# Seven products of quarters instead of eight in two fp32 projections, with sums on GpSimd and exponentials by single heads

## Chip, cores and metric

One NeuronCore of a Trainium2 chip. The metric is the device time in microseconds (us) of the whole kernel, the median of several runs. The engines run side by side and each takes its instructions strictly in its own order: TensorE (PE in the profile; its weight loads PEld) multiplies matrices into PSUM, VectorE is DVE, ScalarE is ACT, GpSimd is POOL, and SyncE (SP) issues most DMA transfers. GpSimd works on SBUF alone; VectorE and ScalarE read PSUM too.

## What is computed

A gated transformer block over 4096 tokens (2 batches of 2048) of width 512: cross-attention with 16 heads of 32 to 77 context tokens, then a feed-forward layer with simulated int8 rounding.

```python
def _L0_xattn_ref(query, key, value, Wq, bq, Wk, bk, Wv, bv, Wo, bo):
    q = proj(query, Wq, bq)          # y = x @ W.T + b, split into 16 heads
    k = proj(key, Wk, bk)
    v = proj(value, Wv, bv)
    scores = jnp.einsum('bhqd,bhkd->bhqk', q, k) / jnp.sqrt(jnp.float32(D_K))
    attn = jax.nn.softmax(scores, axis=-1)
    ctx = jnp.einsum('bhqk,bhkd->bhqd', attn, v)
    return ctx.transpose(0, 2, 1, 3).reshape(B, Sq, D_MODEL) @ Wo.T + bo

def _qlinear(x2d, w, b):             # round(x / sx) @ round(w / sw).T, scaled back
    ...

x = x + tanh(g_xattn) * _L0_xattn_ref(_layernorm(x), ctx, ctx, ...)
x = x + tanh(g_ffn) * _L0_ffn_ref(_layernorm(x), w1, b1, w2, b2)   # _qlinear, gelu, _qlinear
```

`sx` is the largest magnitude of the whole layer input, so the feed-forward half can't begin before all tokens have passed the attention half.

## The kernel before

**Blocks and steps.** The tokens are cut into 8 blocks of 512 (index `i`), each of 4 tiles of 128 (`t`). The 16 heads form 4 groups of 4 (`g`). The attention half is a loop over blocks and, in each, 8 steps `s`: step `s` belongs to group `s // 2` and to one half (256 tokens) of the block. It is software-pipelined by two steps. In step `s` the kernel issues, in this order:

- `apply_v` in even steps (L404): the shares of the group before times the values, into PSUM, copied to `cT` by ScalarE (L412);
- `scores` for two steps ahead (L352) into `ps` (two banks, two buffers), with the maximum over each head (`mx`, L361) and the subtraction of it (`e`, L363) on VectorE;
- `transpose_a` (L395): the shares of this step, transposed in two tiles on TensorE, copied to `aT` by ScalarE (L396);
- `exponential` for two steps ahead on ScalarE, one instruction for 616 columns (L373);
- `shares` for two steps ahead: sum and reciprocal on VectorE (`sm` L380, `rs` L382) and the multiply on GpSimd (L384);
- a quarter of a projection: `project_o` of the block before in even steps (L420), `project_q` of this or the next block in odd ones (L332). A projection of a block is 16 fp32 matmuls of 128x512 for the queries (4 groups of 4) and 16 for the output (4 tiles of 4).

Around these lie the layer norm's statistics of later blocks (`norm_stats`) and of finished ones (`norm2_stats`, `norm2_max`), `add_bias` (L327, GpSimd: the output bias into the residual), `scale_x` (L289, GpSimd: the transposed input from block 2 on times 1/sigma), and weight tasks with fixed steps: the maxima of w1 and w2 (L465), their rounding on ScalarE (L481) and conversion to bf16 on VectorE (L489) into `w1q` and `w2q`, which stay in SBUF.

**Order.** In the attention half the program order is kept for TensorE, VectorE and ScalarE (`tc.manual_schedule`, L511); GpSimd's and the DMA queues' order is chosen by the scheduler, with hints (`tc.issue_after`).

**PSUM.** `ps_s` has 2 buffers for scores, `ps_t` 2 for transposes, `ps_p` 2 for all projections and `apply_v`.

**Feed-forward half** (from L720): bf16 matmuls `ph` (L738), gelu on ScalarE, maxima on VectorE; the hidden values are stored to HBM but for the last 10 tiles; then `pf` (L805) from `w2q`. Its inputs are transposed by DMA (L717) one block ahead.

## Time and profile before

| what | value |
|---|---|
| time, median of 3 runs | 638.99 us (638.86 to 639.27) |
| the profiled run's own time | 640.32 us |
| span of the profiled execution | 638.5 us, 8087 instructions |
| attention half up to the first `ph` | 404.9 us |
| fp32 matmuls of the output projections, L420 | 115.1 us busy, 264 records |
| fp32 matmuls of the query projections, L332 | 86.6 us + 29.3 us busy |
| mean granted TensorE clock | 0.991 |

Times are in us unless marked ns. An fp32 matmul leaves two records, one for each pass. In a line of the timeline the first number is the start from the span's begin, the second the length, then engine, source line, operation, result and operands, shape, and count; in brackets the idle time before it and what ended it. In a line of a group the numbers after the bar are busy us, mean ns of one, idle us of the engine before them and what ended that. "busy" of TensorE counts modelled ends of pipelined matmuls, so neighbours overlap in the list.

### The profile page before, as it was taken

How to read it: one execution, taken by the hardware profiler on the slowest of the kernel's cores; microseconds unless marked ns; L12 is line 12 of the kernel's file. 1: busy time of each engine (PE TensorE's matmuls, PEld its weight loads, DVE VectorE, ACT ScalarE, POOL GpSimd, SP SyncE). 2: the span in 40 equal slices, each digit the busy share in tenths (PEclk: the TensorE clock that was granted, in tenths of full speed). 3: DMA queues.
4: the chain of work that ended last, by engine and by line, in shares of the span. 5: the costliest groups of instructions: out<-in, count | busy, mean ns of one | idle time of the engine just before them, and what ended most of it. 6: DMA issues, size and time to landing. Idle time of an engine off the chain costs nothing.

```text
span 638.5 us, 8087 instructions
## 1 busy us (share of the span) xinstructions
PE 615.9 (96%) x2957; PEld 311.5 (49%) x2978; DVE 509.0 (80%) x796; ACT 341.0 (53%) x450; POOL 247.2 (39%) x202
## 2 busy tenths in 40 slices
PE   5999999999999999999999999799999979999997
PEld 5556555455545554555545555344444424444444
DVE  5688777889898997887857787899999789877452
ACT  2255444563434654544344442598989879556510
POOL 2145457465355364273362341000000009998000
PEclk9999999999999999999999999799999989999999
DMA  9921510442520232220000000199999109798932
GB/s 282 371 97 52 119 42 26 114 168 78 136 66 1 84 131 67 82 68 2 16 1 1 1 17 0 51 337 302 346 331 294 20 24 380 271 376 315 399 129 82
DMA packets 50542, 90.66 MB, mean 142 GB/s; under 512 B 22139, under 2 KB 26491, under 8 KB 44872
## 3 DMA queue, kind: packets, MB, share of 16 engines
q1 hardware_dynamic: 49400, 89.48, 42.8%
q10 hardware_dynamic: 1104, 0.69, 0.4%
q8 instruction: 23, 0.38, 0.2%
q14 instruction: 15, 0.12, 0.1%
HBM read 55.01 MB, written 31.47 MB: 135 GB/s over the span
## 4 chain that ended last, share of the span: by engine, by line
PE 81%; DVE 15%; ACT 1%; POOL 1%; issue 1%; DMA 1%; DVEq 0%
PE ph L738 17%; PE pf L805 17%; PE po L420 13%; PE pq L332 13%; PE pta L395 8%; PE ps L352 6%; PE pc L404 4%; DVE e L363 2%; DVE mx L361 2%; DVE sm L380 1%; DVE st_a L163 1%; DVE max_w L465 1%; PE pk L226 1%; DVE xmax L445 1%; PE pvv L250 1%; DVE x L430 1%
## 5 line engine op out<-in xcount | busy, mean ns | idle before, releaser
L384 POOL TENSOR_TENSOR e<-e,rs 128x616 f32<-128x616 f32 x64 | 81.7, 1277 | 164.4 <-DVE rs L382 77.2
L396 ACT COPY aT<-pta 77x512 f32<-77x512 f32 x128 | 68.2, 583 | 99.4 <-PE pta L395 99.4
L420 PE MATMUL po<-wo_sb,cT 128*128 128x512 f32 (+1 forms) x264 | 115.1, 580 | 0.0
L805 PE MATMUL pf<-w2q,hq 128*128 128x512 bf16 (+1 forms) x518 | 112.0, 376 | 2.9 <-DVE hq L208 2.1
L738 PE MATMUL ph<-xqT,w1q 128*128 128x512 bf16 x501 | 112.0, 383 | 2.6 <-DVE xqT L208 1.8
L746 ACT ACTIVATE G<-ph,b1s,s 128x512 f32<-128x512 f32 x128 | 99.4, 777 | 13.8 <-PE ph L738 2.9
L332 PE MATMUL pq<-xT,wq_sb 128*128 128x512 f32 x192 | 86.6, 593 | 0.2 <-POOL xT L289 0.2
L756 DVE TENSOR_REDUCE hmax<-G 128x1 f32<-128x1024 f32 (+1 forms) x65 | 77.0, 1198 | 7.2 <-ACT G L746 7.1
L805 PEld LDWEIGHTS <-hq 128*128 128x128 bf16 x528 | 51.9, 99 | 62.9 <-DVE hq L208 3.0
L738 PEld LDWEIGHTS <-w1q 128*128 128x128 bf16 x512 | 50.6, 99 | 63.9 <-issue 4.9
L380 DVE TENSOR_REDUCE sm<-e 128x8 f32<-128x616 f32 x64 | 50.3, 787 | 25.9 <-ACT e L373 25.9
L420 PEld LDWEIGHTS po<-wo_sb,cT 128*128 128x128 f32 x264 | 47.8, 190 | 47.5 <-issue 46.2
L395 PE MATMUL pta<-ident,e 128*77 128x128 f32 x512 | 70.2, 280 | 0.6 <-POOL e L384 0.6
L373 ACT ACTIVATE e<-e 128x616 f32<-128x616 f32 x64 | 45.9, 718 | 44.2 <-DVE e L363 42.0
L361 DVE TENSOR_REDUCE mx<-ps 128x8 f32<-128x616 f32 x64 | 50.6, 791 | 17.2 <-PE ps L352 16.9
L395 PEld LDWEIGHTS pta<-ident,e 128*77 128x77 f32 x512 | 55.6, 147 | 11.4 <-issue 9.4
L798 ACT ACTIVATE Gb<-Gb,inv_h 128x2048 f32<-128x2048 f32 x22 | 43.6, 1999 | 32.4 <-DMA Gb<-h 32.4
L352 PEld LDWEIGHTS ps<-kb,qT 64*128 64x128 f32 x512 | 36.0, 186 | 46.9 <-ACT qT L340 23.1
L819 POOL TENSOR_TENSOR x<-x,b_sb 128x512 f32<-128x512 f32 x32 | 57.2, 1823 | 0.1
L363 DVE TENSOR_TENSOR e<-ps,mx 128x616 f32<-128x616 f32 x64 | 51.2, 800 | 6.7 <-DVE mx L361 0.5
L332 PEld LDWEIGHTS pq<-xT,wq_sb 128*128 128x128 f32 x192 | 34.5, 190 | 35.0 <-issue 33.5
L827 DVE SCALAR_TENSOR_TENSOR x<-pf,s,x 128x512 f32<-128x512 f32 (+1 forms) x33 | 23.7, 730 | 34.4 <-PE pf L805 28.4
(101 smaller groups left out, 666.2 us busy)
## 6 DMA issues: line engine op xcount, KB each, us to landing
h<-G SPq DMA_DIRECT2D x22, 1024.0 KB, 6.0
Gb<-h SPq DMA_DIRECT2D x22, 1024.0 KB, 7.9
out_y<-x SPq DMA_DIRECT2D x31, 256.0 KB, 3.2
x<-in_x SPq DMA_DIRECT2D x7, 1024.0 KB, 7.4
xT<-in_xT SPq DMA_DIRECT2D x6, 1024.0 KB, 5.5
raw_w<-in_w2T SPq DMA_DIRECT2D x6, 1024.0 KB, 5.5
raw_w<-in_w1T SPq DMA_DIRECT2D x4, 1024.0 KB, 12.5
rrow<-row SPq DMA_DIRECT2D x6, 256.0 KB, 4.8
```

Of the source, the lines that this page charges most:

```text
L332: nc.tensor.matmul(pq, wq_sb[:, kc, g * P : (g + 1) * P], (xnT if i < 2 else xT_sb)[i][:, kc, :], start=(kc == 0), stop=(kc == KC - 1),)
L352: nc.tensor.matmul(ps[:, q, u * RK : (u + 1) * RK], qT[i, g][r, t * P : (t + 1) * P], kblk[i // NBB][r, g, :], start=True, stop=True,)
L361: nc.vector.tensor_reduce(mx, sc, AX.X, ALU.max)
L363: nc.vector.tensor_tensor(e.rearrange("p u (q r k) -> p q u r k", q=NR, r=RT), sc, mx[:, :, :, :, None].to_broadcast([P, NR, 2, RT, NK]), ...
L384: return nc.gpsimd.tensor_tensor(e4, e4, rs[:, :, :, None].to_broadcast([P, 2, HG, NK]), ALU.mult).ins
L395: nc.tensor.transpose(pt[:NK, j, :], es[i, s][:, u, j, :], ident)
L396: nc.scalar.copy(aT[i, g][:, :, t * P : (t + 1) * P], pt[:NK, :, :])
L420: nc.tensor.matmul(po[i, t, c.start][:, : c.stop - c.start], cT[i, g][:, t * P : (t + 1) * P], wo_sb[:, g, c], start=(g == 0), stop=(g == ...
L738: nc.tensor.matmul(ph[u], w1q[:, kc, fc * P : (fc + 1) * P], cur[:, kc, :], start=(kc == 0), stop=(kc == KC - 1),)
L746: nc.scalar.activation(G[:, 2 * v + u, :], ph[u], AF.Gelu, bias=b1s[:, fc : fc + 1], scale=s1,)
L756: nc.vector.tensor_reduce(hmax[:, k + u : k + u + 1], G[:, 2 * v + u : 2 * v + u + n, :], AX.XY, ALU.max, apply_absolute_value=True,)
L805: nc.tensor.matmul(po[t, c.start][:, : c.stop - c.start], hq[:, fc, t * P : (t + 1) * P], w2q[:, fc, c], start=(fc == 0), stop=(fc == FC - 1),
```

## The change

**Products of quarters.** For the query projections of blocks 2 to 7 and the output projections of blocks 0 to 6, the 512x512x512 product is written as seven products of 256x256x256 quarters (Strassen's algorithm in Winograd's form) instead of eight. `product` issues the four fp32 matmuls of 256 columns of one of them. Units 0, 2, 4, 6 add up in one PSUM bank, units 1, 3, 5 in another; after each unit the running sum is read out: for the queries (`unit_q`) by ScalarE with the bias (units 0, 2, 3, 6) or by VectorE as an addition to what is there (1, 4, 5), for the output (`unit_o`, `add_unit`) by VectorE into the residual. The next unit of a bank has to wait for that reading.

The sums of quarters that feed the products are made on GpSimd: `sums_x` and `sums_c` (four each for every block, 128x512), `sums_wq` and `sums_wo` (four each, once). The units stand in tables by step (`plan`; `second` for block 1, `begin` for block 0, `end` for block 7). `("o", n)` is output unit n of the block before, `("O", 0)` that of this block, `("q", n)` query unit n of the next; `p` and `P` are old `project_q` calls. The last unit of a step has its addition at the start of the next step (`waiting`).

**Exponentials.** The subtraction on VectorE is dropped. VectorE multiplies the maxima by -SCALE (`nmx`), and ScalarE takes the exponential of each head and tile straight from PSUM with that as its bias, eight instructions of 77 columns for a step instead of one of 616. So the scores' PSUM buffer is read until the exponentials end.

**Moved with it.** `apply_v` writes to `ps_t` instead of `ps_p`; `ps_p` becomes two banks used in turn. Statistics and maxima of the norms, centring of wq, `load_x` and `spread_rstd` change their steps. `w2q` is no longer kept through the attention half: its four converted pieces pass through `xqT0` to HBM (`w2_dram`), and one DMA of 2 MB brings them back at the start of the feed-forward half, ahead of the first transposes in SP's queue. GpSimd joins the engines whose program order is kept.

```diff
+    w2_dram = rows.tile([P, FC, D], BF16, tag="w2", name="w2_dram", bufs=1)
...
+        def sums_c(i, n):
+            a11, a21 = (quarter(cT[i, 0], 0, r) for r in range(2))
+            s = ct_s[i, n] = piece(f"cs{i}_{n}")
+            if n == 3:
+                combine(s, a11, a21, ALU.subtract)
+                return
+            a12, a22 = (quarter(cT[i, 1], 0, r) for r in range(2))
+            if n == 1:
+                combine(s, a21, a22, ALU.add)
+            elif n == 2:
+                combine(s, ct_s[i, 1], a11, ALU.subtract)
+            else:
+                combine(s, a12, ct_s[i, 2], ALU.subtract)
+
+        def product(ps, a, b, more=False):
+            for m in range(2):
+                for c in range(2):
+                    nc.tensor.matmul(
+                        ps[:, m * H : (m + 1) * H],
+                        a[:, c, m * P : (m + 1) * P],
+                        b[:, c, :],
+                        start=(m + c == 0 and not more),
+                        stop=(m + c == 2),
+                        skip_group_check=True,
+                    )
...
+            if n in (0, 2, 3, 6):
+                for m in range(2):
+                    g = 2 * r + m
+                    nc.scalar.activation(
+                        q[:, m, :], ps[:, m * H : (m + 1) * H], AF.Identity, bias=bq_sb[:, g : g + 1]
+                    )
+            else:
+                nc.vector.tensor_tensor(q, ps.rearrange("p (m t) -> p m t", m=2), q, ALU.add)
+
+        def unit_o(i, n):
+            pa, pb = chain(("o", i))
+            ct = [cT[i, c] for c in range(2)]
+            a, b = (
+                (quarter(ct[0], 0, 0), quarter(wo_sb, 0, 0)),
+                (quarter(ct[1], 0, 0), quarter(wo_sb, 1, 0)),
+                (ct_s.get((i, 2)), wo_t[:, 1]),
+                (ct_s.get((i, 1)), wo_t[:, 0]),
+                (ct_s.get((i, 3)), wo_t[:, 2]),
+                (ct_s.get((i, 4)), quarter(wo_sb, 1, 1)),
+                (quarter(ct[1], 0, 1), wo_t[:, 3]),
+            )[n]
+            product(pb if n in (1, 3, 5) else pa, a, b, more=n in (2, 4, 5, 6))
...
-            e = work.tile([P, 2, GK], F32, tag="e", name=f"e{n}", bufs=3)
-            nc.vector.tensor_tensor(
-                e.rearrange("p u (q r k) -> p q u r k", q=NR, r=RT),
-                sc,
-                mx[:, :, :, :, None].to_broadcast([P, NR, 2, RT, NK]),
-                ALU.subtract,
-            )
+            nmx = small.tile([P, NR, 2, RT], F32, tag="nmx", name=f"nmx{n}")
+            nc.vector.tensor_scalar(nmx, mx, -SCALE, None, ALU.mult)
...
-            return nc.scalar.activation(e, e, AF.Exp, scale=SCALE).ins
+            for u in range(2):
+                for q in range(NR):
+                    for r in range(RT):
+                        j = q * RT + r
+                        last = nc.scalar.activation(
+                            es[i, s][:, u, j * NK : (j + 1) * NK],
+                            sc[:, q, u, r, :],
+                            AF.Exp,
+                            bias=nmx[:, q, u, r : r + 1],
+                            scale=SCALE,
+                        )
...
-            pc = ps_p.tile([P, TB], F32, tag="pp", name=f"pc{i}_{g}")
+            pc = ps_t.tile([P, TB], F32, tag="pt", name=f"pc{i}_{g}")
...
+            dst = w1q[:, :, j * TB : (j + 1) * TB] if name == "w1" else xqT0
             nc.vector.tensor_scalar(dst, wraw[name, j], MAGIC, None, ALU.subtract)
+            if name == "w2":
+                nc.sync.dma_start(w2_dram[:, j * KC : (j + 1) * KC, :], xqT0)
...
+        plan = {
+            0: [("o", 1)],
+            1: [("o", 2), ("o", 3)],
+            2: [("o", 4), ("o", 5)],
+            3: [("o", 6), ("q", 0)],
+            4: [("q", 1), ("q", 2)],
+            5: [("q", 3), ("q", 4)],
+            6: [("q", 5)],
+            7: [("q", 6), ("O", 0)],
+        }
+        begin = {1: [("p", 2)], 3: [("p", 3)], 5: [("P", 0)], 6: [("P", 1)], 7: [("P", 2)]}
+        end = {s: [("o", s + 1)] for s in range(6)}
...
+                if waiting:
+                    add_unit(*waiting)
+                    waiting = None
                 if ahead[0] < NB:
                     scores(*ahead)
...
+                if i > 0 and s == 1:
+                    sums_c(i - 1, 2)
+                d = 2 if i == 1 else 1
+                if i > 0 and more and s == d + 3:
+                    sums_x(i + 1, 2)
...
                 if ahead[0] < NB:
-                    last = shares(*ahead)
+                    shares(*ahead)
+                for n, (kind, unit) in enumerate(units.get(s, ())):
...
+                if i > 0 and s == 0:
+                    sums_c(i - 1, 1)
+                if i > 0 and s == 1:
+                    sums_c(i - 1, 4)
+                if more and i > 0:
+                    if d <= s < d + 2:
+                        for kc in range(2):
+                            scale_x(i + 1, 2 * (s - d) + kc)
+                    if s == d + 2:
+                        sums_x(i + 1, 3)
+                        sums_x(i + 1, 1)
+                    if s == d + 4:
+                        sums_x(i + 1, 4)
+                if more and s == 7:
+                    sums_c(i, 3)
+                t = s - NT if i == 0 else s // 2
+                if t >= 0 and (i == 0 or s % 2 == 0):
+                    add_bias(i, t)
...
+    w2q = late.tile([P, FC, D], BF16, name="w2q")
+    nc.sync.dma_start(w2q, w2_dram)
```

## The prediction

> **What bounds the kernel now.** I read the engine totals, then the chain of work that ended last, then the busy time of one block of the attention half, and last the timeline inside it.
>
> ```profile
> PE 615.9 (96%) x2957; PEld 311.5 (49%) x2978; DVE 509.0 (80%) x796; ACT 341.0 (53%) x450; POOL 247.2 (39%) x202
> ...
> PE 81%; DVE 15%; ACT 1%; POOL 1%; issue 1%; DMA 1%; DVEq 0%
> ```
>
> TensorE is busy nearly throughout and holds 81% of the chain. One block, from one `apply_v` of step 0 to the next:
>
> ```profile
> 253.50:299.00 45.50, 45.50 (x227) 23.31 (x226) 36.48 (x65) 21.25 (x33) 21.93 (x20) 1.00 0.17 53
> ```
>
> The columns after the length are TensorE, its weight loads, VectorE, ScalarE, GpSimd: TensorE has no gap in 45.5 us, VectorE is at 80%, GpSimd at 48%. Two steps in order of time:
>
> ```profile
> 248.31 0.80 PE L352 MATMUL ps<-kb,qT 64*128 64x154 f32 x8
> 249.03 1.10 PE L395 MATMUL pta<-ident,e 128*77 128x128 f32 x8
> 249.15 0.80 DVE L361 TENSOR_REDUCE mx<-ps 128x8 f32<-128x616 f32 x1
> 249.97 3.60 PE L332 MATMUL pq<-xT,wq_sb 128*128 128x512 f32 x8
> 250.05 0.80 DVE L363 TENSOR_TENSOR e<-ps,mx 128x616 f32<-128x616 f32 x1
> 250.88 0.72 ACT L373 ACTIVATE e<-e 128x616 f32<-128x616 f32 x1
> 251.63 0.80 DVE L380 TENSOR_REDUCE sm<-e 128x8 f32<-128x616 f32 x1 [0.78 <-ACT e L373]
> 252.47 0.20 DVE L382 RECIPROCAL rs<-sm 128x8 f32<-128x8 f32 x1
> 252.84 1.22 POOL L384 TENSOR_TENSOR e<-e,rs 128x616 f32<-128x616 f32 x1 [1.81 <-DVE rs L382]
> ```
>
> Starts are first. From scores to the GpSimd multiply it is 4.53 us (248.31 to 252.84), and nobody waits for it, since those shares are transposed two steps later. So TensorE bounds, and what shortens it pays only as long as nothing else makes it wait.
>
> **The change, part by part.**
>
> *Products.* Four 512-column matmuls take 3.44 us in the chain (249.97 to the next work is 3.53), 0.86 each, so a projection of 16 is 13.76. A 256-column one is half, 0.43; the 128x256 row of L420 gives 3.6 us for 8, 0.45. A product of four is 1.72, seven are 12.04. Query of blocks 2 to 7 and output of blocks 0 to 6 make 13 projections: 13 x 1.72 = -22.4 us of TensorE (-15 at 0.45). I take 0.43.
>
> *Exponentials.* VectorE loses the subtraction (64 x 0.80) and gains `nmx`; ScalarE gets eight 128x77 instructions for one of 0.72. The nearest row is the 32x77 one with a bias column:
>
> ```profile
> L242 ACT ACTIVATE kb<-pk,bk_sb 32x77 f32<-32x77 f32 x8 | 2.5, 318 | 6.2 <-DVE kb L244 6.2
> L396 ACT COPY aT<-pta 77x512 f32<-77x512 f32 x128 | 68.2, 583 | 99.4 <-PE pta L395 99.4
> L170 DVE TENSOR_SCALAR ve_f<-mean 128x2 f32<-128x2 f32 x13 | 7.8, 600 | 0.5
> L170 DVE TENSOR_SCALAR ve_a<-mv 128x4 f32<-128x4 f32 x7 | 1.2, 169 | 0.2
> ```
>
> Two copies of 583 ns end within 1.07 us, so neighbours overlap by 0.095: eight take 8 x 0.223 + 0.095 = 1.88 us. Ends: 1.5 (from the 203 ns of the one-column `warm`, plus 0.064 for 77 elements by the slope of the copies) and 2.5 (no overlap). I take 1.88. The Trainium skill ("ScalarE: Activation LUTs", What ACT_TABLE_LOAD costs) gives 280 ns plus 0.833 ns an element with a bias pointer and 93 ns of overlap; an estimate from it is 2.10 us, which would add about 3 us to the whole sum. `nmx` is 0.17 by the `ve_a` row, 0.60 by `ve_f`: the same instruction, which there sits until a GpSimd instruction ends (253.48 to 254.08, GpSimd's multiply being at work from 252.84). New latency from scores to multiply: 0.84 + 0.91 + 0.20 + 1.88 + 0.03 + 0.83 + 0.37 = 5.06 us, the unchanged links from the timeline above. ScalarE gains 512 x 0.223 - 46 = 68 us and stays under 80% of a block; VectorE's account is -51 + 11 (`nmx`) + 18 query additions at 0.69 (the 77x512 `vb` row) + 21 more output additions at 0.73 = -12 us. Neither is the bound by its total.
>
> *GpSimd sums: where TensorE now waits.* 60 new sums of 128x512 at 1.27 us (the L327 and L289 rows): 76 us, mostly in blocks 1 to 6, GpSimd from 48% to some 70%. The total fits; the order does not. In steps 0 and 1 of a block GpSimd's queue reads: multiply of this step's scores, first sum (`sums_c` 1), `add_bias`, second sum (`sums_c` 2). TensorE's queue from the same scores on: transposes, unit 1, scores, transposes, unit 2, and unit 2 reads the second sum. GpSimd is done 5.06 + 1.18 + 1.23 + 1.23 + 1.27 = 9.97 us after the scores began. TensorE arrives after 0.73 + 0.93 + 1.81 + 0.73 + 0.93 = 5.13. It waits 4.9 us, and all behind it does (unit 3, `apply_v`, the next scores). Both chains begin at the same scores, so no slack built up elsewhere helps. It happens in blocks 2 to 7; in block 1 unit 2 comes a step later.
>
> *Second wait.* Scores 1 of the next block (step 7) read the query sum that VectorE writes after unit 5 (step 6). VectorE gets to it only after that step's maximum, the eight exponentials, sum and reciprocal: 4.69 + 0.12 + 0.69 + 0.1 = 5.6 us after the scores; TensorE has 0.73 + 0.93 + 1.81 = 3.5 of work: 2.1 us of wait. In step 5 the query addition and two `norm2_stats` follow the reciprocal and make VectorE 0.5 late: 2.6. Blocks 2 to 6; about 0.8 in block 1.
>
> *Third.* Unit 2 of the queries waits for `sums_x` 2, fourth behind a multiply: 9.97 against 9.66 of TensorE work, 0.3 us.
>
> So a block 2 to 6 needs 42.0 + 4.9 + 2.6 + 0.3 = 49.8 us (45.5 - 2 x 1.72 = 42.0). Before, these five ran from 115.89 to 344.55 in the list of the chain: 228.7. Now 249: **+20.5**.
>
> *Port.* Each `nmx` can sit behind a GpSimd instruction, up to 1.2 us. Following GpSimd's queue through a block, it is at work when `nmx` is due in steps 0, 4, 5 and 6, which feed the two waits: about +1.9 a block, 6 blocks, **+11** (0 to +24).
>
> *Clock.* TensorE now stands still 11 times for 2.6 us or more.
>
> ```profile
> 396.91 2.72 PE L666 MATMUL px<-ident,xs 128*128 128x128 f32 x16
> 402.27 0.79 PE L185 MATMUL pg_x<-diag_x,ones 128*128 128x128 f32 x2 [2.65 <-DVE diag_x L178]
> 404.89 1.44 PE L738 MATMUL ph<-xqT,w1q 128*128 128x512 bf16 x3 [1.82 <-DVE xqT L208]
> ```
>
> and the busy time in stretches of 4 us, the third column from the end being the granted clock:
>
> ```profile
> 404.00:408.00 4.00, 2.89 (x7) 1.13 (x8) 3.93 (x10) 1.21 (x2) 0.56 (x1) 0.50 0.00 0
> 408.00:412.00 4.00, 4.00 (x18) 1.67 (x16) 4.00 (x7) 3.56 (x5) 0.00 (x0) 0.87 0.23 39
> ```
>
> After standing 2.65 and 1.82 us TensorE runs at clock 0.50 until about 409, 6.8 us; after 2.17 and 1.75 at 519 it is 3.4 us. A 3.4 us stretch at half clock loses 1.7 us. Ends: nothing, and 3.4 for each of 11 waits, 37. I take 1.7 for six long waits and half for five short: **+14**. The Trainium skill ("TensorE: Matmul & The Clock Gate", Part 1: The HAM clock gate) wants an idle window of about 3.4 us before the clock halves; by it only the six long waits count, an estimate of +10. It speaks against this change either way.
>
> *The rest.* Block 0 gets a fifth projection (+3.4); block 1 has 47.0 us of TensorE work against 46.6, the 0.8 and more VectorE work: +3 (0 to 6). In block 7 shorter projections are met by the 4.9 wait and VectorE's chain: 0 (-5 to +2). The weight maxima and roundings of blocks 2 to 5 lie on VectorE (L465: 1.19 each), where it waits anyhow; what spills over: +3 (0 to 10). w2 goes out in four writes and comes back in one read of 2 MB ahead of the transposes in SP's queue; 1024 KB land in 5.5 to 6.0 us, and 409.5 to the first use of the second transposes near 420 is cover: 0 (up to 5).
>
> Sum on the 638.5 us span: 20.5 + 11 + 14 + 3.4 + 3 + 0 + 3 = +55, 693. The profiled run reports 640.32, the median of the runs is 638.99; the difference on the median gives 694, and I forecast **692**.
>
> **Rivals.**
> - *The waits alone* (no port, clock or spill): 639 + 20.5 + 3.4 = 663, and 657 at the short exponentials; 652 to 672. For it: every link is in the rows. Against it: the half clock is in this trace.
> - *VectorE and ScalarE fall behind step after step*: port waits at 4 us a block and the clock twice as dear, 712 and up. For it: VectorE's chain in steps 4 to 6 has no slack. Against: it is idle during the long wait.
> - *TensorE stays the bound, faster*: 639 - 22.4 = 617. One mechanism decides, the wait of output unit 2 in step 1: the gain survives only if GpSimd's second sum ends within 5.1 us of the scores, not 10. Even at no cost for the exponentials (8.1) it does not; only sums at a third of 1.27 would do it. The break-even lies where that wait falls to about 1.5 us and the second to none.
> - *The effects cancel*, 638 to 652: the lower end of each.
>
> **How the numbers follow.** My case (672 to 712) 62%, waits alone 20%, falling behind 11%, faster 5%, cancelling 2%. The range 660 to 716 reaches into the two slower neighbours and leaves out about 2 in 10. Runs of before agree within 0.07%, so 0.2% is about what can be told from no change. Faster 0.05, same 0.01, slower 0.94.
>
> **What would show it.** TensorE idle before output unit 2, about 5 us in each of blocks 2 to 7, released by GpSimd's `cs`; idle before scores, released by VectorE's `qT`, some 2 to 4 us five times; eight exponentials in 1.9 us; clock 0.5 after the long waits; blocks 2 to 6 at 50 to 56 us. It is wrong if those blocks run at 42 to 45 us, or if `cs` is ready before TensorE asks.

## The result and the profile after

The changed kernel takes 737.66 us (median; 736.01 to 741.93) where the kernel before takes 638.92: a ratio of 1.156, 95% interval 1.150 to 1.161. That is 98.7 us slower; the forecast was 53 us slower, 692 us, and its range ended at 716. The profiled execution has a span of 734.2 us against 638.5. Its engine totals, its granted clock in 40 slices, and the chain of work that ended last:

```profile
PE 632.3 (86%) x3269; PEld 391.5 (53%) x3290; DVE 526.5 (72%) x834; ACT 412.4 (56%) x922; POOL 324.7 (44%) x261
...
PEclk9989999989999889989998998898999999999999
...
PE 56%; DVE 21%; ACT 11%; POOL 9%; issue 2%; DMA 0%; ACTq 0%; DVEq 0%; POOLq 0%
```

TensorE has lost its place as the bound: 81% of the chain before, 56% now. Although it has less to multiply, it is busy 16.4 us longer (615.9 before), and it stands idle 101.9 us instead of 22.6. Both have to be explained. Busy time by stretches, block 4 (with weight tasks) and block 5 (nearly without); columns as before, the clock third from the end:

```profile
259.88:323.48 63.60, 48.30 (x273) 36.02 (x272) 44.57 (x76) 33.31 (x95) 35.69 (x28) 0.89 0.29 96
323.48:378.82 55.34, 46.01 (x274) 34.85 (x273) 37.56 (x69) 29.94 (x93) 32.41 (x28) 0.94 0.10 34
```

Each was 45.5 us before. From one first `apply_v` to the next the eight blocks (0 to 7) grew by 11.1, 11.6, 16.8, 12.4, 18.1, 9.8, 11.5 and 3.9 us; the feed-forward half by 0.5. What TensorE waited for (us in total, times, the longest):

```profile
PE oa L432 <- POOL cs L369: 33.9, 7, 6.3
PE ps L508 <- DVE qT L474: 19.7, 6, 5.9
PE qa L432 <- POOL xt L369: 11.3, 5, 3.2
...
PE pta L559 <- ACT cT L577: 6.6, 6, 2.4
```

These are the three waits of the forecast and one more. The first in order of time, block 4, the end of step 0 and step 1:

```profile
263.44 1.83 ACT L530 ACTIVATE e<-ps,nmx 128x77 f32<-128x77 f32 x8
...
264.36 0.80 PE L508 MATMUL ps<-kb,qT 64*128 64x154 f32 x8
...
265.08 1.10 PE L559 MATMUL pta<-ident,e 128*77 128x128 f32 x8
265.30 0.80 DVE L544 TENSOR_REDUCE sm<-e 128x8 f32<-128x616 f32 x1 [0.79 <-ACT e L530]
...
266.50 1.99 POOL L548 TENSOR_TENSOR e<-e,rs 128x616 f32<-128x616 f32 x1 [3.19 <-ACT aT L560]
...
268.46 1.25 POOL L369 TENSOR_TENSOR cs<-cT,cT 128x512 f32<-128x512 f32 x1
...
269.68 1.26 POOL L337 TENSOR_TENSOR x<-x,bo_sb 128x512 f32<-128x512 f32 x1
...
270.90 1.44 POOL L369 TENSOR_TENSOR cs<-cs,cT 128x512 f32<-128x512 f32 x1
...
272.39 1.22 PE L432 MATMUL oa<-wo_t,cs 128*128 128x256 f32 x2 [6.21 <-POOL cs L369]
```

GpSimd's queue runs as foreseen: multiply, first sum, bias, second sum; only then can TensorE go on, 6.2 us late. The eight exponentials take 1.83 us (1.88 foreseen). Behind such a wait, the busy time in stretches of 4 us:

```profile
268.00:272.00 4.00, 0.00 (x0) 0.00 (x0) 3.93 (x6) 2.16 (x9) 4.00 (x4) 0.75 0.89 286
272.00:276.00 4.00, 3.61 (x9) 2.89 (x10) 0.84 (x2) 1.55 (x1) 3.29 (x4) 0.50 0.28 107
```

The clock falls while TensorE stands still and is still 0.50 when it begins again: its next product takes some 3.6 us instead of 1.73. The trace records 90.8 us at half clock (13.1 before), of which 2.0 (2.1) lie behind the last instruction; TensorE was busy in 75.4 of them (7.8 before). If half of the busy time at half clock is lost, that is 37.7 against 3.9 us, **33.8 us more** (an estimate from the two busy times). With that the account of the 95.7 us of span is 79.3 (idle) + 33.8 (clock) - 17.4. The last term is not measured here, it is what is left, and stands for less work; `best3` below gives 17.5 for it in another way.

The new and lengthened instructions of the softmax, as groups (busy us, mean ns of one, idle before them and what ended it), first the sum in the kernel before, then three groups of the changed one:

```profile
L380 DVE TENSOR_REDUCE sm<-e 128x8 f32<-128x616 f32 x64 | 50.3, 787 | 25.9 <-ACT e L373 25.9
```

```profile
L530 ACT ACTIVATE e<-ps,nmx 128x77 f32<-128x77 f32 x512 | 116.5, 340 | 51.9 <-DVE nmx L519 51.6
...
L544 DVE TENSOR_REDUCE sm<-e 128x8 f32<-128x616 f32 x64 | 50.8, 793 | 78.7 <-ACT e L530 78.3
...
L519 DVE TENSOR_SCALAR nmx<-mx 128x8 f32<-128x8 f32 x64 | 32.3, 504 | 2.2
```

VectorE waits 78.3 us for the exponentials (25.9 before), ScalarE 51.6 us for `nmx`, and `nmx`, 0.17 us at its shortest, takes 0.50 on average. Of the 64 the 24 that meet no GpSimd instruction take 0.17 us, and all 30 that take more than 0.3 us end 0.03 us behind the end of a GpSimd instruction. The chain of waits in block 4, steps 2 to 4, is this loop:

```profile
281.76 1.72 ACT e L530 x8
...
283.50 0.81 DVE sm L544
...
284.33 0.20 DVE rs L546
284.54 0.62 DVE x L496
285.15 2.14 DVE xqT L650
287.29 0.66 DVE x L496
287.95 0.72 DVE mx L517
...
288.69 0.99 DVE nmx L519
...
289.76 1.83 ACT e L530 x8
```

ScalarE, then VectorE for 6 us (a weight task of 2.14 in it), then ScalarE again, in the time of one step. While ScalarE works VectorE stands, and what it has still to do comes later.

### The profile page after: what moved, and what is told of

It reads as the page before. It is cut to its first block, busy times and chain, and to the rows that moved or that the text cites. A ratio compares the mean times of both kernels' runs of the same rounds, so it can differ in the third digit from the quotient of the medians.

```text
span 734.2 us, 9354 instructions
## 1 busy us (share of the span) xinstructions
PE 632.3 (86%) x3269; PEld 391.5 (53%) x3290; DVE 526.5 (72%) x834; ACT 412.4 (56%) x922; POOL 324.7 (44%) x261
## 4 chain that ended last, share of the span: by engine, by line
PE 56%; DVE 21%; ACT 11%; POOL 9%; issue 2%; DMA 0%; ACTq 0%; DVEq 0%; POOLq 0%
PE ph L968 15%; PE pf L1035 15%; ACT e L530 8%; PE oa L432 5%; PE pta L559 4%; PE qa L432 4%; PE ps L508 3%; DVE sm L544 3%; PE ob L432 3%; PE pq L342 3%; POOL cs L369 2%; DVE mx L517 2%; DVE nmx L519 2%; POOL e L548 2%; ACT aT L560 2%
## 5 line engine op out<-in xcount | busy, mean ns | idle before, releaser
L548 POOL TENSOR_TENSOR e<-e,rs 128x616 f32<-128x616 f32 x64 | 79.4, 1240 | 194.1 <-DVE rs L546 137.3
L530 ACT ACTIVATE e<-ps,nmx 128x77 f32<-128x77 f32 x512 | 116.5, 340 | 51.9 <-DVE nmx L519 51.6
L560 ACT COPY aT<-pta 77x512 f32<-77x512 f32 x128 | 69.8, 586 | 74.9 <-PE pta L559 74.6
L544 DVE TENSOR_REDUCE sm<-e 128x8 f32<-128x616 f32 x64 | 50.8, 793 | 78.7 <-ACT e L530 78.3
L559 PE MATMUL pta<-ident,e 128*77 128x128 f32 x512 | 77.6, 296 | 8.9 <-ACT cT L577 6.6
L559 PEld LDWEIGHTS pta<-ident,e 128*77 128x77 f32 x512 | 60.2, 157 | 23.3 <-issue 9.7
L508 PE MATMUL ps<-kb,qT 64*128 64x154 f32 x512 | 52.6, 326 | 20.9 <-DVE qT L474 19.7
L432 PE MATMUL oa<-wo_t,cs 128*128 128x256 f32 x112 | 37.3, 492 | 33.9 <-POOL cs L369 33.9
L1026 POOL TENSOR_SCALAR b_sb<-b_sb,s 128x512 f32<-128x512 f32 x1 | 3.5, 3497 | 123.1 <-issue 123.1
L577 ACT COPY cT<-pc 128x512 f32<-128x512 f32 x32 | 19.1, 598 | 62.6 <-PE pc L568 62.5
L432 PEld LDWEIGHTS oa<-wo_t,cs 128*128 128x128 f32 x112 | 26.6, 250 | 40.0 <-POOL cs L369 35.5
```

The lines of the kernel that those rows point to most:

```text
L432: nc.tensor.matmul(ps[:, m * H : (m + 1) * H], a[:, c, m * P : (m + 1) * P], b[:, c, :], start=(m + c == 0 and not more), stop=(m + c == 2 ...
L508: nc.tensor.matmul(ps[:, q, u * RK : (u + 1) * RK], qT[i, g // 2][r, g % 2, t * P : (t + 1) * P], kblk[i // NBB][r, g, :], start=True, sto ...
L530: last = nc.scalar.activation(es[i, s][:, u, j * NK : (j + 1) * NK], sc[:, q, u, r, :], AF.Exp, bias=nmx[:, q, u, r : r + 1], scale=SCALE,)
L544: nc.vector.tensor_reduce(sm, e4, AX.X, ALU.add)
L548: return nc.gpsimd.tensor_tensor(e4, e4, rs[:, :, :, None].to_broadcast([P, 2, HG, NK]), ALU.mult).ins
L559: nc.tensor.transpose(pt[:NK, j, :], es[i, s][:, u, j, :], ident)
```

## The experiments

Three theories. **A**: TensorE's operands come late by the order on GpSimd and VectorE, and the array then runs at half clock. **B**: the longer loop of VectorE and ScalarE in each step sets the time. **C**: small VectorE instructions (`nmx`, `xf`, integers) are held up by GpSimd's work beside them. Times are medians; ratios to the kernel before, measured alongside (638.8 to 640.1 us), with 95% intervals.

### One part alone or undone

`e_whole` takes the exponentials back to the old form: `nmx` out, VectorE subtracts into SBUF, one exponential of 616 columns (8 of 77; the forecast below has 1232).

```diff
-            nc.vector.tensor_scalar(nmx, mx, -SCALE, None, ALU.mult)
+            nc.vector.tensor_tensor(e..., sc, mx..., ALU.subtract)
...
-            (eight activations of 77 columns)
+            return nc.scalar.activation(e, e, AF.Exp, scale=SCALE).ins
```

> The change without its part on the exponentials: VectorE subtracts the maxima into SBUF again and ScalarE takes one exponential of 1232 columns, so that the small product on VectorE (nmx) is gone and ScalarE loses about 0.9 us a step. Theory A (GpSimd and VectorE deliver operands of the products late, and the array then works at half clock): the operands are as late as before, 725 to 750 us. Theory B (the longer serial loop VectorE, ScalarE, VectorE of each step sets the time): 690 to 715 us, and VectorE's idle time behind the exponentials falls from 78 us to about 26. Theory C (VectorE's small SBUF instructions wait for a port that GpSimd holds): nmx's 32 us go and 0.75 us of subtraction a step comes for it, 715 to 735 us.

706.1 us, 1.103 (1.100 to 1.106): 31.5 us less. VectorE's idle time behind the exponentials fell to 20.6 us. This is B's span.

`before_single` puts only the eight exponentials and `nmx` into the kernel before.

```diff
-            nc.vector.tensor_tensor(e..., sc, mx..., ALU.subtract)
+            nc.vector.tensor_scalar(nmx, mx, -SCALE, None, ALU.mult)
...
-            return nc.scalar.activation(e, e, AF.Exp, scale=SCALE).ins
+            (eight activations of 77 columns, bias=nmx[...], scale=SCALE)
```

> The kernel before with the eight single exponentials and nmx alone, no product of quarters. Theory A: TensorE keeps its order and nearly its time, 636 to 650 us. Theory B: the loop is longer by some 0.6 us in 64 steps and decides, 660 to 685 us. Theory C: little GpSimd work lies beside it, nmx stays near 0.2 us; 636 to 650 us as under A.

653.5 us, 1.021 (1.019 to 1.023): 13.4 us, between the forecasts. No product of quarters and no GpSimd sum is in it, so the exponentials cost something by themselves. `nmx` takes 0.55 us on average here too, and C was wrong to expect 0.2: all 31 that take more than 0.3 us end 0.03 us behind a GpSimd instruction, of work that was always there. The wait list of VectorE shows nearly the same time behind the exponentials as in the changed kernel:

```profile
DVE sm L388 <- ACT e L374: 74.5, 47, 2.4
```

`cs_early` issues the two sums behind the longest wait ahead of the multiply.

```diff
+                if i > 0 and s == 0:          # ahead of shares(*ahead)
+                    sums_c(i - 1, 1)
+                    sums_c(i - 1, 2)
-                if i > 0 and s == 1:
-                    sums_c(i - 1, 2)
```

> The changed kernel with the two sums cs_1 and cs_2 issued on GpSimd ahead of the multiplication of step 0, instead of behind it and in step 1. Theory A: TensorE's 33.9 us behind cs_2 go, with most of the half clock behind them (7 waits of up to 3.4 us lost); 685 to 705 us. Theory B: TensorE then stands at the next scores or transposes instead, 722 to 738 us. Theory C: the same GpSimd work holds the same port, 700 to 715 us (the wait goes, the stretched VectorE stays).

707.6 us, 1.106 (1.102 to 1.109): 30.1 us less. The wait is gone from the list but for 1 us, and the waits for `qT` (19.6) and `xt` (12.5) are as before; the one for `cT` grew from 6.6 to 12.4, and `nmx` from 0.50 to 0.62 us on average. Time at half clock fell from 90.8 to 57.0 us. That is just beyond A's span and in C's: the wait is gone, and part of the gain came back as another.

`no_sums` leaves all sums of `sums_x` and `sums_c` out and takes unsummed quarters, so its outputs are not those of the block.

```diff
         def sums_x(i, n):
+            xt_t[i, n] = {1: b12, 2: b22, 3: b22, 4: b21}[n]
+            return
...
         def sums_c(i, n):
+            ct_s[i, n] = quarter(cT[i, int(n > 2)], 0, n % 2)
+            return
```

> The changed kernel without the eight sums of each block (products take unsummed quarters in their place, so the outputs are not those of the reference; all matrix products and additions remain). Theory A: cs, xt and most of the half clock go, and qT stays (19.7 us and its clock); 655 to 680 us. Theory B: 700 us or more. Theory C: as A, and also nmx, xf and the integers on VectorE come back to the durations of before, which makes the blocks with weight tasks as short as the others; 640 to 660 us.

687.5 us, 1.074 (1.072 to 1.077), between A and B. Even with no sums of these two kinds it is 47 us slower than the kernel before (640.1 beside it). So GpSimd's order is only half of the matter, and C's prediction that the durations come back fails: `nmx` still takes 0.52 us on average, beside multiplies, scalings and biases, which were all there before.

### The sums of a step moved past the next maxima

`defer` issues the sum, reciprocal and multiply of a step one step later, right behind the next scores' maxima. The shares are not transposed before the step after that, so the move is free in principle, and VectorE never needs the exponentials of its own step.

```diff
                 if ahead[0] < NB:
                     scores(*ahead)
+                if pending:
+                    shares(*pending)
+                pending = ahead if ahead[0] < NB else None
...
-                if ahead[0] < NB:
-                    shares(*ahead)
```

`before_single_defer` does it in the kernel before with single exponentials; `defer_early` does it in the changed kernel with `cs_1` and `xt_2` ahead of the multiply and `cs_2` right behind; `early_whole` is `cs_early` with the old exponentials. The order in `defer_early`, behind the scores:

```diff
+                if i > 0 and s == 0:
+                    sums_c(i - 1, 1)
+                if i > 0 and more and s == d + 3:
+                    sums_x(i + 1, 2)
+                if pending:
+                    shares(*pending)
+                pending = ahead if ahead[0] < NB else None
+                if i > 0 and s == 0:
+                    sums_c(i - 1, 2)
```

> The kernel before with the single exponentials, and each step's sums, reciprocals and multiplication issued one step later, right behind the next step's maxima, so that VectorE never stands behind the exponentials of its own step. Theory B (the serial loop VectorE, ScalarE, VectorE costs the 13.4 us that the single exponentials cost alone): 636 to 643 us, with VectorE's 75 us of waiting for e nearly gone. Theory C (the lengthened nmx and the other work on VectorE cost them): 648 to 656 us as without the move.

647.6 us, 1.012 (1.007 to 1.017). The median is between the two forecasts (the profiled execution is the longest of the runs, 649.9 us), so the blocks have to decide. Two of them, 3 and 4:

```profile
168.08:213.79 45.71, 45.71 (x228) 23.68 (x227) 38.52 (x75) 27.58 (x88) 23.00 (x21) 1.00 0.31 67
213.79:259.28 45.49, 45.49 (x225) 23.30 (x224) 35.43 (x66) 32.73 (x91) 22.81 (x20) 1.00 0.31 99
```

TensorE has no gap again (49.3 and 47.1 us without the move), and VectorE's wait for `e` is 1.7 us. So the middle blocks no longer pay for the exponentials. The move did two things at once, though: `nmx` now meets a GpSimd instruction only 9 times instead of 44 and is short again. Without the move, and with it:

```profile
L363 DVE TENSOR_SCALAR nmx<-mx 128x8 f32<-128x8 f32 x64 | 35.2, 550 | 2.2
...
L363 DVE TENSOR_SCALAR nmx<-mx 128x8 f32<-128x8 f32 x64 | 13.1, 204 | 2.2
```

So how much of the gain is the wait for `e` (B) and how much the shorter `nmx` (C) this run doesn't separate. The move itself costs 3 us each in block 0 (75.3 against 72.2) and block 7 (64.0 against 60.9), where no later work hides the multiply.

> The changed kernel with the same move of the sums and the multiplication by one step and nothing else. Theory B: the loop cost about the 31 us that the whole exponential gave back, and the addition for q unit 5 is no longer behind it (19.7 us of TensorE behind qT go); the wait for cs_2 stays; 685 to 710 us. Theory A: only qT goes, and cs_2 is as late as before or later; 715 to 730 us. Theory C: 720 to 738 us.

708.7 us, 1.109 (1.105 to 1.114): 29.0 us less, at the upper edge of B's span. The wait for `qT` fell from 19.7 to 8.8 us, the one for `cs` only from 33.9 to 28.4; `nmx` fell here too, from 0.50 to 0.37 us on average.

> Both: the move, and on GpSimd cs_1 ahead of the multiplication of step 0, cs_2 right behind it, xt_2 ahead of that of its step. Theories A and B together: both costs go, with the half clock behind them: 650 to 675 us. If the gains overlap: 680 to 700 us. What stays in any case is block 0's 11 us and the weight tasks.

661.9 us, 1.035 (1.031 to 1.039): 75.7 us less, more than the 59.1 of the two moves alone (xt_2's wait also fell, to 3.8). Blocks 5 and 6 take 43.8 and 44.0 us, for the first time less than the 45.5 of the kernel before.

> The changed kernel with cs_1 and cs_2 early and with the exponential of a whole step as before. If the two gains (30.1 us and 31.5 us) are separate: 675 to 682 us. If they overlap: 690 to 705 us.

676.8 us, 1.059 (1.056 to 1.063): 60.9 less, where the two alone gave 30.1 and 31.5. The two gains are separate and nearly add.

### What `nmx` costs

`after_min` and `defer_min` need no `nmx`: K and its bias are multiplied by -SCALE when they are placed, VectorE takes a minimum, which is already the bias, and the exponential has scale -1.

```diff
-            nc.vector.tensor_reduce(mx, sc, AX.X, ALU.max)
-            nc.vector.tensor_scalar(nmx, mx, -SCALE, None, ALU.mult)
+            nc.vector.tensor_reduce(mx, sc, AX.X, ALU.min)
...
-                    nc.vector.tensor_scalar(dst, pk[r, :NK], bias, None, ALU.add)
+                    nc.vector.tensor_scalar(dst, pk[r, :NK], -SCALE, bias, ALU.mult, ALU.add)
```

> The changed kernel without nmx: the factor -SCALE is put into K and its bias once, VectorE takes minima in place of maxima, and the eight exponentials take these as their bias with scale -1. Theory C (nmx, stretched from 0.17 us to as much as 1.29 us by GpSimd, is a main part of the loss): its 32 us of VectorE lie in the serial loop, so 700 to 715 us. Theories A and B (order, not nmx): 718 to 733 us, since at most the loop's 0.5 us a step goes where VectorE is the last to come.

720.9 us, 1.127 (1.124 to 1.131): 16.8 us less for 32.3 us of VectorE. In A's and B's span: C is a part, not the main one.

> The kernel with both moves (sums one step later, GpSimd's order mended; 661.9 us) and without nmx in the same way. If VectorE bounds blocks 2 to 4 (33 to 44 us busy a block of 48 to 51): each of them loses 2 to 4 us, 648 to 656 us in all. If GpSimd and the waits for q unit 5 bound them: 658 to 663 us.

645.4 us, 1.011 (1.007 to 1.014): 16.5 us less once more, beyond the forecast. Block 3 fell from 48.5 to 43.8, block 4 from 50.8 to 47.8.

### The half clock by itself

`after_fill` keeps every wait of the changed kernel, but TensorE multiplies in it: 14 products whose result nobody reads, ahead of output unit 2 in step 1 of blocks 2 to 7.

```diff
+                if 1 < i and s == 1:
+                    for n in range(14):
+                        nc.tensor.matmul(wide[i, 2][:, n % 2, 2 * RK :], ident,
+                                         wo_sb[:, n % 4, : 512 - 2 * RK], start=True, stop=True, ...)
```

> The changed kernel, all its waits kept, with 14 matrix products of 128x204 (about 0.35 us each, 4.9 us) put ahead of o unit 2 in step 1 of blocks 2 to 7, into columns of a scores bank that nothing reads. They fill most of the wait of 5.3 to 6.3 us for cs_2 and are done by then; the wait is as long, only not idle. If half clock behind idle time is a large part of the loss (up to 3.4 us behind each of the six waits, and by it later operands of VectorE's loop too): 715 to 727 us. If half clock mostly falls on time that is waited through anyway: 733 to 740 us. If the products delay the path themselves: above 740 us.

721.7 us, 1.130 (1.127 to 1.133): **16.0 us less by 30 us more of work.** TensorE's order of time in block 3:

```profile
205.85 5.00 PE L756 MATMUL ps<-wo_sb,ident 128*128 128x204 f32 x28
211.33 1.99 PE L432 MATMUL oa<-wo_t,cs 128*128 128x256 f32 x8 [0.48 <-POOL cs L369]
```

Output unit 2 starts 0.5 us after the useless products and takes 1.99 us, where in the changed kernel it takes 3.42 behind 5.29 us of standing. Busy time at half clock fell from 75.4 to 50.9 us, 12.3 us less lost, and the gain is larger than that: the lost time lay on the path. These are six waits of one kind; what the half clock behind the others costs was not tried.

### What remained, and a version that beats both

`defer_order` mends further places: wq's centring and wo's sums in GpSimd's idle time of block 0, q unit 5 earlier (order 1, 0, 3, 2, 5, 4, 6), `xt_2` right behind `xt_1`. `all` is that without `nmx`.

```diff
-            3: [("o", 6), ("q", 0)],
-            4: [("q", 1), ("q", 2)],
-            5: [("q", 3), ("q", 4)],
-            6: [("q", 5)],
+            3: [("o", 6), ("q", 1)],
+            4: [("q", 0), ("q", 3)],
+            5: [("q", 2), ("q", 5)],
+            6: [("q", 4)],
...
+        total = sum_wq()                       # ahead of the loop
...
-                if i == 0 and s == 3:
-                    center_wq(total)
+                if i == 0 and s in (3, 4):
+                    center_wq(mean, 2 * (s - 3))
...
-                if i == 0 and s == 7:
-                    for n in range(3):
-                        sums_wo(n)
+                if i == 0 and s in (1, 2):
+                    for n in range(2):
+                        sums_wo(2 * (s - 1) + n)
...
                         sums_x(i + 1, 1)
+                        sums_x(i + 1, 2)
```

> The kernel with both moves (661.9 us), and with orders mended further: the centring of wq and its sums spread over GpSimd's idle time in block 0, wo's four sums in steps 1 and 2 of block 0, q unit 5 ahead of q unit 4 (units 1, 0, 3, 2, 5, 4, 6), xt_2 right behind xt_1. If block 0's and block 1's losses (7 and 9 us over the kernel before) are GpSimd's queue in these places and the 10.2 us behind qT are the place of unit 5: 640 to 650 us. If they are VectorE's load: 655 to 663 us.

656.1 us, 1.026 (1.023 to 1.029). TensorE no longer waits for `qT`, block 1 fell from 56.0 to 49.5, but 19.0 us of waiting for the multiply came (11.2 before the mend). A part went to the new wait.

> All together: both moves, the mended orders and no nmx. If the shares are separate: 628 to 640 us, which would be the first version with the products of quarters that is not slower than the kernel before. If VectorE's load takes the place of the waits: 645 to 655 us.

641.2 us, 1.003 (1.002 to 1.004): between the forecasts, 20.7 less than `defer_early`.

`best` takes `all`, keeps the sums of block 0 and of the last step of block 7 in their own step, and issues the statistics of X a step later and `xt_4` behind the multiply.

```diff
+                soon = k < 7 or (not more and s == 5)
+                if ahead[0] < NB and not soon:
+                    pending = ahead
...
+                if ahead[0] < NB and soon:     # in the old place
+                    shares(*ahead)
...
-                    steps = (5, 5, 6, 7) if more else (5, 5, 6, 6)
+                    steps = (6, 6, 7, 7) if more else (5, 5, 6, 6)
...
-                    if s == d + 4:
+                if more and i > 0 and s == d + 5:   # behind the multiply
                     sums_x(i + 1, 4)
```

`before_min_defer` has the same exponentials, the same `pending` and `soon` in the kernel before.

> The kernel with all mends (641.2 us), with the sums kept in their own step in block 0 and at the very end of block 7 (where there are no products of quarters to fill, and the move cost 3 us each), the statistics of X one step later and xt_4 behind the multiplication. If blocks 0 and 7 are 3 us each too long by the move and the 0.7 us before the transposes of each step 7 goes: 631 to 637 us, faster than before. If the DVE's load or something else shows: 638 to 643 us.

649.9 us, 1.017 (1.015 to 1.019): a miss, by one place. For block 1 the sum `xt_4` had come too late:

```profile
128.43 3.78 PE L436 MATMUL qb<-xt,wq_sb 128*128 128x256 f32 x8 [6.40 <-POOL xt L373]
```

One wait of 6.4 us and its half clock made block 1 57.4 us long instead of 48.8; the whole kernel lost 8.7 us. Block 0 did not gain (76.6 against 75.2).

> The kernel before with the same exponentials (single heads, minima, no nmx) and the same move of the sums with the same edges, but with whole products. TensorE bounds its blocks at 45.5 us whatever VectorE does: 636 to 641 us. What best is faster than this is what the products of quarters are worth on the same ground. If VectorE's time was what bounded blocks of the kernel before: below 634 us.

641.9 us, 1.006 (1.004 to 1.009), a little above the forecast: blocks 1 to 6 at 45.5 to 46.7, block 7 at 63.8. On the same ground without products of quarters nothing is won. The ground is that of `best`; the later moves (the first steps, the weight tasks) were not tried in the kernel before. They could not win anything in its blocks 2, 4, 5 and 6, where TensorE has no gap in 45.5 us.

`best2` puts `xt_4` back in block 1 and keeps sums in their own step only in the first two steps and at the end; the statistics go back too.

```diff
-                soon = k < 7 or (not more and s == 5)
+                soon = k < 2 or (not more and s == 5)
```

> The kernel with all mends (641.2 us), with xt_4 behind the multiplication from block 2 on (in block 1 where it was), the sums of the first two steps and of the very last step of block 7 kept in their own step. If the waits of up to 3.2 us of TensorE for the multiplication in step 7 and at the end are its place in GpSimd's queue: 633 to 637 us, faster than the kernel before. If blocks 2 to 4 stay at 44 to 48 us because VectorE is full: 638 to 642 us.

639.6 us, 1.000 (0.998 to 1.002): no difference to be told. Blocks 2 and 4 stay at 47.8 and 48.5. The order of time in block 4 on four engines shows why:

```profile
244.50 2.00 ACT L648 ACTIVATE raw_w<-raw_w,inv_w 128x2048 f32<-128x2048 f32 x1
...
249.00 0.88 ACT L474 ACTIVATE qT<-qb,bq_sb 128x256 f32<-128x256 f32 x2
...
249.92 0.69 DVE L478 TENSOR_TENSOR qT<-qa,qT 128x512 f32<-128x512 f32 x1 [4.34 <-ACT qT L474]
...
255.44 1.22 POOL L550 TENSOR_TENSOR e<-e,rs 128x616 f32<-128x616 f32 x1 [1.32 <-DVE rs L548]
...
256.70 1.99 PE L561 MATMUL pta<-ident,e 128*77 128x128 f32 x8 [3.18 <-POOL e L550]
```

ScalarE rounds a weight for 2 us, its copy of a q unit comes behind, VectorE stands 4.3 us in front of its addition, the sums behind it (and a weight conversion of 1.22 us) are late, then the multiply, then TensorE. `best3` moves only such weight tasks:

```diff
-            at(13 + 2 * j, weight_round, "w1", j)
-            at(14 + 2 * j, weight_integers, "w1", j)
+            at(14 + 2 * j, weight_round, "w1", j)
+            at(15 + 2 * j, weight_integers, "w1", j)
...
-        for j, step in (2, 31), (3, 33), (0, 36), (1, 40):
+        for j, step in (2, 32), (3, 34), (0, 38), (1, 40):
```

> best2 (639.6 us) with the roundings of the weights at the ends of even steps alone, where the copies of aT follow on ScalarE and not cT or a q unit, and their integers one step behind. If the place of the tasks on ScalarE holds blocks 2 and 4: each loses 2 to 4 us, 632 to 636 us, faster than the kernel before. If it is their load on VectorE and ScalarE wherever they stand: 638 to 641 us.

**634.3 us, 0.992 (0.990 to 0.995): 0.8% faster than the kernel before**, a small gain, but clear of the spread. Its totals and chain:

```profile
PE 600.2 (95%) x3290; PEld 371.6 (59%) x3290; DVE 485.2 (77%) x771; ACT 409.7 (65%) x922; POOL 327.9 (52%) x261
...
PE 81%; DVE 11%; ACT 3%; POOL 3%; issue 2%; DMA 1%; DVEq 0%; POOLq 0%; ACTq 0%
```

and its blocks 4 and 5:

```profile
214.96:258.50 43.54, 42.80 (x273) 32.49 (x272) 35.71 (x64) 33.10 (x95) 34.33 (x28) 1.00 0.33 103
258.50:302.05 43.55, 42.80 (x274) 32.50 (x273) 34.37 (x63) 29.56 (x93) 34.35 (x28) 1.00 0.30 89
```

Block 4 lost 5 us; block 2 did not (49.3, where `best2` had 47.8). That the whole lies within the forecast is in part luck, since only one of the two blocks moved as foreseen. In block 2 the moved tasks now do what they did in block 4:

```profile
151.62 2.00 ACT L648 ACTIVATE raw_w<-raw_w,inv_w 128x2048 f32<-128x2048 f32 x1
...
157.04 0.69 DVE L478 TENSOR_TENSOR qT<-qa,qT 128x512 f32<-128x512 f32 x1 [4.35 <-ACT qT L474]
...
159.46 1.21 DVE L632 TENSOR_REDUCE max_w<-raw_w 128x1 f32<-128x1024 f32 x1
...
160.59 1.22 DVE L652 TENSOR_SCALAR w1q<-raw_w 128x2048 bf16<-128x2048 f32 x1
...
163.69 1.22 POOL L550 TENSOR_TENSOR e<-e,rs 128x616 f32<-128x616 f32 x1 [3.35 <-DVE rs L548]
```

The multiply waits for VectorE, and TensorE stands 4.31 us for the multiply. No run mends this place. In blocks 4 and 5 TensorE is the bound again, at full clock, with 2.7 us less work a block. Half clock is down to 15.8 us. A block 0 of 74.1 us against 69.3 remains, with a projection more in it, and a block 7 of 52.8 against 60.4, with the work that was moved ahead taken off.

## Why the prediction went wrong

The direction and the places of the three waits were right, the size was not: +55 us of span foreseen, +95.7 found. By the forecast's own steps (the products' -17.4 is what the other two leave of 95.7):

| step | forecast | found |
|---|---|---|
| *Products*, 13 x 1.72 | -22.4 | -17.4 |
| *Clock* | +14 | +33.8 |
| TensorE idle (all other terms: 55 - 14 + 22.4) | +63.4 | +79.3 |

- **Clock: the term that failed most.** I took 1.7 us for six long waits and half of it for five short ones; the upper end, 3.4 for each of 11 waits, was 37. Found: 77.7 us more at half clock, in 18 stretches, blocks 0, 1 and 7 among them, and TensorE was busy in most of that time. `after_fill` alone gives 16.0 us for the six long waits, which I had at 10.2. Short waits can cost as much as long ones: half clock also stands behind waits of 2.41 us (to 174.6 us) and 2.55 (to 236.1), though not behind one of 2.62 (to 298.0). The Trainium skill ("TensorE: Matmul & The Clock Gate", Part 1: The HAM clock gate), which wants an idle window of about 3.4 us and by which I had worked out +10, does not agree with this trace, where the half clock began 2.2 us after TensorE had stopped at 172.2 us.
- **The cover on VectorE: the second.** "Neither is the bound by its total" is true (VectorE 72% of the span; its account of -12 us came out at +17.5, mostly by `nmx` at 32 instead of 11), and it did not help: from the exponentials to the sum VectorE has no other work in its order, and waited 78.3 us there instead of 25.9. I counted the latency once (5.06 us from scores to multiply) and said the weight tasks "lie on VectorE, where it waits anyhow", at +3. It waits at another place, and is at work during TensorE's long waits. `before_single` shows 13.4 us with all products whole; `before_single_defer` shows blocks 3 to 6 back at 45.5 to 45.7 once the wait has something behind which to lie (and `nmx` is short again). In the changed kernel the whole exponential gives 31.5 us, the move 29.0, `nmx` by itself 16.8.
- **Waits one and two** had the right place and engines: `cs` 33.9 us (6 x 4.9 = 29.4 foreseen), `qT` 19.7 (13.8). The wait for `cs` is 5.3 us in blocks 3, 5, 6 and 7; it is 6.2 and 6.3 in blocks 4 and 2, where the multiply took 1.99 us beside VectorE's integers instead of 1.22 (I had 1.18).
- **Wait three** was mis-sized: 0.3 us a block foreseen, 11.3 in all found, up to 3.2. I had weighed 9.97 against 9.66 us, a balance of two long sums in which whatever is late on VectorE or GpSimd falls on one side.
- **Port**: +11 (0 to 24). The mechanism is shown: the long `nmx` end with a GpSimd instruction. They lengthened `nmx` by 21 us in all (32.3 against 64 x 0.17). What that costs alone no run tells; `after_min`, which takes all of `nmx` away, gives 16.8 us.
- **The rest**: block 0 was foreseen at +3.4 and grew 11.1, block 1 at +3 and grew 11.6, block 7 at 0 and grew 3.9. In block 0, to which the centring of wq was moved, TensorE stands 2.5 us for GpSimd's `wq_total` (to 48.1 us) and then works 6.8 us at half clock.
- **Products**: `best3`, where nothing hides it, has 42.80 us of TensorE work a block against 45.50: 1.35 us a projection, 17.5 for 13. The forecast's other end (-15, from the 0.45 row) was nearer.
- **Rivals.** "VectorE and ScalarE fall behind step after step", 712 and up at 11%, has the right size, and one of its two conditions came true: the clock cost 2.4 times the +14. The other, port waits at 4 us a block, isn't shown: without any `nmx` 16.8 us are won in all. I had held against it that VectorE is idle during the long wait; in the six long waits of blocks 2 to 7, 33.7 us, VectorE is at work for 33.2. "TensorE stays the bound, faster" was tied to one wait; `cs_early` takes that wait away and stays at 707.6 us. It took the move, the sums' order, `nmx` and the weight tasks together.

The sum took its terms as independent. The upper ends that I had stated (port 24, clock 37, block 1 6, block 7 2, weight tasks 10, w2 5) with the 20.5 and block 0's 3.4 make 107.9 us, so the 95.7 found lie below them; but blocks 0, 1 and 7 exceed what I had given them, while the clock stays below. That the terms feed each other is my reading: a wait brings the half clock, the half clock makes TensorE later for the next scores, and the loop of VectorE starts from these. `after_fill` agrees with it, since it takes away 12.3 us of lost clock and gains 16.0, but no run follows the loop itself.

Not separated by any run: what w2's way through HBM costs (no wait of TensorE, VectorE, ScalarE or GpSimd for it is in any list, and the feed-forward half grew by 0.5 us).

## What to carry to other kernels

An engine with a low total is no cover if its own queue makes it stand: look in its order for what lies between a producer on another engine and the consumer behind it, and move the consumer past the next independent work. Before work is taken off TensorE, list every operand that will now come from a slower engine, with the queue that it stands in; here seven products for eight paid 0.8% only when all of these queues had been put in order, and cost 15.6% before. Price an idle TensorE with the half clock that follows; here, with many waits, it came near the upper end (33.8 of 37 us).

## What the runs showed of the hardware that was not expected

- Useless work is worth its time: 30 us of products in six waits made the kernel 16.0 us faster, with the next product, in block 3, at 1.99 instead of 3.42 us.
- In the recorded clock, half speed comes in stretches of 3.41 us or twice that and lasts into the work behind. In each of these runs the starts of all its stretches lie whole multiples of 3.413 us apart, to within 0.002 us (in the changed kernel 119.83, 150.55, 174.44: 9 and 7 times). So what a wait costs depends also on where it falls: the wait of 2.41 us has 2.23 of it ahead of the boundary at 174.44, the one of 2.62 is cut by the boundary at 297.3 into 1.94 and 0.68. How much standing it takes was not tried.
- A VectorE instruction of 8 elements a row took 0.17 us alone and up to 1.29 beside GpSimd work (0.50 on average over all 64), and its long ones end with the GpSimd instruction beside them. Of the 64 multiplies on GpSimd, 62 took 1.21 to 1.23 us and two 1.99, both of these beside VectorE's conversion of a weight: both sides pay.
